# A low-rank adapter and a feed-forward network on one core: the adapter's second products in float32r from two parts

## The chip, the core and the metric

The kernel runs on one core of a Trainium2 chip. The core has TensorE (PE: products of matrices, with a separate weight load, PEld), VectorE (DVE), ScalarE (ACT), GpSimd (POOL) and SyncE (SP), which here only issues transfers. Data lie in SBUF, 128 partitions wide; products go to PSUM, 8 banks of 128 partitions by 512 float32. The engines run at the same time and wait for each other through semaphores; each one works off its own instructions in order.

The metric is the device time of one execution in microseconds, and for a kernel the median of several runs.

## The reference, cut to what matters

```
# x: (8, 256, 1024) float32; one adapter number per batch of 256 rows
B_sel = B[adapter_ids]; A_sel = A[adapter_ids]          # rank 16
Bx  = einsum('bnr', x, B_sel)                            # 1024 -> 16
c   = einsum('bno', Bx, A_sel)                           # 16 -> 1024, times 1.0
x_dq = fp8(clip(c / in_scale, -448, 448)) * in_scale
gate_out = x_dq @ (gate_w * gate_w_scale).T              # 1024 -> 2752
up_out   = x_dq @ (up_w * up_w_scale).T
hidden   = silu(gate_out) * up_out
h_dq     = fp8(clip(hidden / down_in_scale)) * down_in_scale
return x + h_dq @ (down_w * down_w_scale).T              # 2752 -> 1024
```

The weights are float32 that hold fp8 values. The adapter's two products decide what fp8 value each element of c rounds to, so they are made to float32's accuracy.

## The kernel before, in words

The 2048 rows (8 batches of 256) are four blocks t = 0 to 3 of 512 columns, two batches each, everything transposed: the 1024 features lie on 8 slices k of 128 partitions. The 2752 hidden features are 22 groups c of 128 (the last is half a group).

- **x and weights.** `load_x` (L381), `load_b` (L366), `load_a_two` (L373), the loop on `a_four` (L420) and `load_gate_up` (L391) issue transfers, nearly all on SP's queue, in the program's order: x of block 0 with its B and A; weights of groups 0 to 4 (`NFIRST = 5`), 1 MB each; B of block 1, x of block 1 in two pieces (7 slices, then 1), A of block 1 in four pieces of 16 rows; x of blocks 2 and 3, each followed by two B; the four A of blocks 2 and 3, 16 rows each; the rest. Eight semaphores are used in turn for these transfers.
- **B's product** (`times_b`). x is the moving operand, in float32, and one B of 16 columns (loaded as 32 columns, so the neighbours come along) the weights. Four products at a time use the four column groups of the array. Blocks 0 and 1 are done alone, with two batches, each halved, as the four (`two_times_b`: 128 columns each); blocks 2 and 3 together, with their four batches (`four_times_b`: 256 columns).
- **bm.** B's result is copied to SBUF. For blocks 0 and 1, bm has two versions of 64-row halves (`bm[:, other]`): VectorE copies one half of the rows, ScalarE the other, twice each (L517), so that each batch's A finds all columns. For blocks 2 and 3 it is one copy on VectorE (L557).
- **A's product** (`two_times_a`, `four_times_a`). Four products at a time use the four row groups of the array, with 32 rows of weights (16 of A, 16 of zeros) and 128 columns in block 1, and 16 rows and 256 columns in blocks 2 and 3. A call handles 4 accumulators of a PSUM bank each (two slices k by 256 columns); when they are complete, `round_to` evicts them to fp8 as xg, two on ScalarE (L529) and two on VectorE (L527).
- **Gate and up** (`gate_up(c, t)`): 8 products of 512 columns for gate, 8 for up (with `turns` in alternating pieces of two slices), then Silu on ScalarE (L610) and a fused multiply on VectorE (L611), which writes hid. `between` puts something between two of the 16 products. Groups 0 to 4 take block 0 first, then block 1, then blocks 2 and 3; groups 5 to 21 take all four blocks at a time.
- **Order.** TensorE's products go through `multiply` (L471) and keep the program's order, as do the copies to bm of blocks 0 and 1 and the checks `note_low_bits` and `note_squares` on ScalarE. Silu, fused multiply and the evictions are free: the framework's scheduler places them.
- **Around the change**, in the order of TensorE: `gate_up(4, 0)` is interrupted before its 13th product by block 1's B (`two_times_b(1)`), ends with its last 4, and `two_times_a(1)` follows, then `gate_up(0, 1)` in turns. `gate_up(3, 1)` is interrupted after 8 products by `four_times_b`, then `four_times_a` for the first two pairs of chunks (`pairs` 0, 1), `gate_up(4, 1)` interrupted after 8 by `four_times_a` for pairs 2 and 3; then groups 0 to 4 for blocks 2 and 3.
- **PSUM** is one pool of 8 banks, used by all of these in turn: a new accumulator waits for the readers of the one whose bank it takes.
- **Down** follows from group 22 on: 8 slices of the output, each with 21 products of hid and the tail, added to x and stored.

Of the kernel before, what the change touches and what calls it, by code (L numbers as in the profile page):

```python
# [8 lines left out]

F32 = mybir.dt.float32  # L10
BF16 = mybir.dt.bfloat16
FP8 = mybir.dt.float8e4
U16 = mybir.dt.uint16
I32 = mybir.dt.int32
AF = mybir.ActivationFunctionType
ALU = mybir.AluOpType
AX = mybir.AxisListType

P = 128
T = 2048  # L20
SEQ = 256
NB = 8
H = 1024
I = 2752
R = 16
NH = H // P
NI = (I + P - 1) // P
# [5 lines left out]
NFIRST = 5  # L33

BROW = NH * R + 8

KS = NH // 2
# [246 lines left out]
def adaln_ffn(  # L284
# [4 lines left out]
    aT: bass.AP,  # L289
    bT: bass.AP,  # L290
    a8: bass.AP,
    b8: bass.AP,
    w_gu: bass.AP,
    w_d: bass.AP,
# [3 lines left out]
    nc = tc.nc  # L298
    const = ctx.enter_context(tc.tile_pool(name="const", bufs=1))
    psum = ctx.enter_context(  # L300
        tc.tile_pool(name="psum", bufs=8, space=bass.MemoryType.PSUM)
    )
# [19 lines left out]
    kept = ctx.enter_context(tc.tile_pool(name="kept", bufs=1))  # L322
    wpool = ctx.enter_context(tc.tile_pool(name="w", bufs=5))
    outs = ctx.enter_context(tc.tile_pool(name="outs", bufs=3))
    hid = [kept.tile([P, T], FP8, name=f"hid{c}") for c in range(NI - 1)]


    hid_tail = kept.tile([P, 2, TB], BF16, name="hid_tail")
# [8 lines left out]
    with ExitStack() as fast:  # L337
# [17 lines left out]
        b_four = lora.tile([P, 4 * BROW + R], F32, name="b_four")  # L355
        a_four = lora.tile([P, H], F32, name="a_four")
        nc.gpsimd.memset(a_two[0], 0.0)
        nc.vector.memset(a_two[1], 0.0)
        for b, n in ((b_two[0], 2), (b_two[1], 2), (b_four, 4)):
            nc.vector.memset(b[:, n * BROW :], 0.0)  # L360

# [3 lines left out]
        def load_b(b, i, adapter, queue):  # L365
            queue.dma_start(  # L366
                out=b[:, i * BROW : (i + 1) * BROW], in_=b8[bass.ds(adapter * P, P), :]
            )

        def load_a_two(t, j, adapter, queue=nc.sync):  # L370
            for g in range(2):
                row = 32 * (2 * g + j) + R * j
                queue.dma_start(  # L373
                    out=a_two[t][row : row + R],
                    in_=a8[bass.ds(adapter * 2 * R + g * R, R), :],
                )

        def load_x(t, k):
            piece, first = x_of(x4, t, k)
# [27 lines left out]
        adapters = [adapter_of(2 + q, nc.sync) for q in range(6)]  # L407
        for j in range(2):
            load_b(b_two[1], j, adapters[j], nc.sync)
        for k in (0, 7):  # L410
            load_x(1, k)
        for j in range(2):
            load_a_two(1, j, adapters.pop(0))

        for t in (2, 3):
            load_x(t, 0)
            for q in (2 * t - 4, 2 * t - 3):
                load_b(b_four, q, adapters[q], nc.sync)
        for q in range(4):
            nc.sync.dma_start(  # L420
                out=a_four[32 * q : 32 * q + R], in_=aT[bass.ds(adapters[q] * R, R), :]
            )


        sc = b_two[0][:, NH * R : BROW]
# [44 lines left out]
        def multiply(*args, **kwargs):  # L470
            tc.keep_in_program_order(nc.tensor.matmul(*args, **kwargs))  # L471

        def pass_time(to, n, size=P):

            for i in range(n):
                multiply(
                    to[:, :size],
                    lhsT=zeros[:, :P],
                    rhs=zeros[:, :size],
                    start=(i == 0),  # L480
                    stop=(i == n - 1),
                )

        def times_b(bx, b, n, quads, between=None):


            for k in range(NH):
                for q, (i, row, t, cols) in enumerate(quads):
                    at = i * BROW + k * R - row
                    multiply(  # L490
                        bx[q][32 * q : 32 * (q + 1)],
                        lhsT=b[:, at : at + 32],
                        rhs=xs[t][:, k, cols],
                        start=(k == 0),
                        stop=(k == NH - 1),
                    )
                if between:
                    between(k)

        def two_times_b(t, between=None):  # L500


            n = SEQ // 2
            quads = [
                (j, R * j, t, slice(at, at + n))
                for half in range(2)
                for j in range(2)
                for at in (j * SEQ + half * n,)
            ]
            bx = [psum.tile([P, n], F32, tag="ps", name=f"bx{half}") for half in range(2)]  # L510
            times_b([bx[q // 2] for q in range(4)], b_two[t], n, quads, between)
            bm = lora.tile([P, 2, n], F32, tag="bm2", name="bm2", bufs=2)
            for other in range(2):
                for half, copy in enumerate((nc.vector.tensor_copy, nc.scalar.copy)):
                    to = half ^ other
                    tc.keep_in_program_order(
                        copy(  # L517
                            bm[64 * to : 64 * (to + 1), other],
                            bx[half][64 * half : 64 * (half + 1)],
                        )  # L520
                    )
            return bm

        def round_to(to, c, engine):
            scale = inv[:, GATE_IN : GATE_IN + 1]
            if engine is nc.vector:
                nc.vector.tensor_scalar(to, c, scale, None, ALU.mult, saturate=False)  # L527
            else:
                nc.scalar.activation(to, c, AF.Copy, scale=scale, saturate=False)  # L529

        def two_times_a(t, bm):


            n = SEQ // 2
            for part in range(2):
                cs = [psum.tile([P, 2, SEQ], F32, tag="ps", name=f"c{q}") for q in range(4)]
                for other, i in product(range(2), range(2)):
                    for q in range(4):
                        rows = slice(32 * q, 32 * (q + 1))
                        multiply(  # L540
                            cs[q][:, i, bass.ts(q // 2 ^ other, n)],
                            lhsT=a_two[t][rows, bass.ts(2 * part + i, P)],
                            rhs=bm[rows, other],
                            start=True,
                            stop=True,
                        )
                for q in range(4):
                    k = KS * part + 2 * (q // 2)
                    to = xg[t][:, k : k + 2, bass.ts(q % 2, SEQ)]
                    round_to(to, cs[q], nc.vector if q % 2 else nc.scalar)  # L550

        def four_times_b():
            quads = [(q, 0, 2 + q // 2, bass.ts(q % 2, SEQ)) for q in range(4)]
            bx = psum.tile([P, SEQ], F32, tag="ps", name="bx")
            times_b([bx] * 4, b_four, SEQ, quads)
            bm = lora.tile([P, SEQ], F32, tag="bm", name="bm", bufs=2)
            nc.vector.tensor_copy(bm, bx)  # L557
            return bm

        def four_times_a(bm, pairs):  # L560
            for i in pairs:
                cs = [psum.tile([P, 2, SEQ], F32, tag="ps", name=f"c{q}") for q in range(4)]
                for k in range(2):
                    for q in range(4):
                        rows = slice(32 * q, 32 * q + R)
                        multiply(
                            cs[q][:, k],
                            lhsT=a_four[rows, bass.ts(2 * i + k, P)],
                            rhs=bm[rows],
                            start=True,  # L570
                            stop=True,
                        )
                for q in range(4):
                    to = xg[2 + q // 2][:, 2 * i : 2 * i + 2, bass.ts(q % 2, SEQ)]
                    round_to(to, cs[q], nc.vector if q % 2 else nc.scalar)
# [5 lines left out]
        def gate_up(c, t, turns=(NH,), between=None):  # L581
# [23 lines left out]
            if tail:  # L605
                to = lora.tile([P, 2 * TB], FP8, tag="bm", name="tail", bufs=2)[half_of(t), :TB]
            else:
                to = hid[c][:, cols]
            g = work.tile([P, TB], F32, tag="g", name="g")
            nc.scalar.activation(g[rows], gates, AF.Silu, scale=gate_s[: gates.shape[0]])  # L610
            nc.vector.scalar_tensor_tensor(  # L611
                to,
                in0=ups,
                scalar=up_by_down[rows],
                in1=g[rows],
                op0=ALU.mult,
                op1=ALU.mult,
                saturate=False,
            )
            if tail:  # L620
                nc.vector.tensor_copy(hid_tail[half_of(t), t // 2], to)
            if t == (NTB - 1 if c < NFIRST else 1):
# [10 lines left out]

        warm = psum.tile([P, TB], F32, tag="ps", name="warm")
        pass_time(warm, 16, TB)
        bm = two_times_b(0, lambda k: pass_time(warm, 4) if k == 6 else None)
        pass_time(warm, 7)
        two_times_a(0, bm)
        gate_up(0, 0, turns=(2, 2, 2, 2))
        for c in range(1, NFIRST - 1):  # L640
            gate_up(c, 0)
        bms = []
        gate_up(NFIRST - 1, 0, between=(12, lambda: bms.append(two_times_b(1))))
        two_times_a(1, bms[0])
        gate_up(0, 1, turns=(2, 2, 2, 2))
        for c in range(1, NFIRST - 2):
            gate_up(c, 1)
# [238 lines left out]
```

## Time and profile before

| what | value |
| --- | --- |
| median of 3 runs | 475.71 us (475.62 to 475.85) |
| profiled execution, span from the first to the last instruction | 474.0 us |
| TensorE busy | 469.6 us, 99% |
| A's products of blocks 0 and 1, 128 records together | 4.3 us busy |
| A's products of blocks 2 and 3, 64 records | 4.1 us busy |
| B's products of blocks 0 and 1, 128 records; of 2 and 3, 64 records | 4.3 and 3.7 us busy |
| eviction of c, one of 128x512 | 0.688 us on ScalarE (L529), 0.745 on VectorE (L527) |
| copy to bm, 64x128 | 0.283 us on VectorE, 0.262 on ScalarE (L517) |
| copy to bm, 128x256 | 0.425 us on VectorE (L557) |
| Silu; fused multiply | 0.681 us (L610); 0.751 (L611) |
| GpSimd busy | 1.0 us in 7 instructions, all in the first 1.55 us |
| TensorE clock granted | 1.000 |

The median of the runs is 1.7 us more than the profiled span. A float32 product is recorded twice by the profiler, as two records. In the timeline a row gives the start, the time to the end of the last instruction merged into it, the engine, the line, the operation with its tiles and shapes, how many, and in brackets the idle time before it with what ended it. Ends of products are modelled, so neighbouring rows of PE overlap a little: the starts are to be read. Busy time of an engine that is not on the chain of waits costs nothing by itself.

### The profile page before, as it was taken

To read this page: it belongs to the slowest core of one execution; us is meant where nothing else is said; L and a number is where in the kernel's file an instruction comes from. 1 tells how busy PE (TensorE), PEld (TensorE's weight loads), DVE (VectorE), ACT (ScalarE), POOL (GpSimd) and SP (SyncE) were. 2 spreads that over 40 slices of the span, in tenths; PEclk is the share of its full clock that TensorE was granted. 3 is DMA by queue.
4 is the path that set the end of the run, shared out by engine and by line. 5 is a ranking of instruction groups with operands and counts; after the bars stand their busy time and mean duration, and the time that the engine had idled before them with its cause. 6 is when DMAs were issued, how large, how long until landed. Compare 5 with 4: busy or idle time off the path is not lost.

```text
span 474.0 us, 6007 instructions
## 1 busy us (share of the span) xinstructions
PE 469.6 (99%) x2514; PEld 217.1 (46%) x2514; DVE 105.6 (22%) x163; ACT 192.5 (41%) x249; POOL 1.0 (0%) x7
## 2 busy tenths in 40 slices
PE   8999999999999999999999999999999999999997
PEld 5454544444444444444444444444444444444444
DVE  2332521212212121222212121232120121031031
ACT  2332438995555745443354544359212022021000
POOL 0000000000000000000000000000000000000000
DMA  8995023322222112222210121133335255163031
GB/s 316 416 406 153 1 90 115 153 89 90 89 89 90 54 45 80 90 89 89 90 57 36 41 62 56 61 100 106 115 135 162 66 184 160 28 212 110 3 116 67
DMA packets 13781, 53.45 MB, mean 113 GB/s; under 512 B 1650, under 2 KB 2930, under 8 KB 10802
## 3 DMA queue, kind: packets, MB, share of 16 engines
q1 hardware_dynamic: 13536, 52.86, 31.8%
q8 instruction: 21, 0.34, 0.3%
q10 hardware_dynamic: 210, 0.14, 0.1%
q14 instruction: 14, 0.11, 0.1%
HBM read 44.60 MB, written 8.39 MB: 112 GB/s over the span
## 4 chain that ended last, share of the span: by engine, by line
PE 96%; DMA 2%; ACTq 0%; ACT 0%; issue 0%; DVE 0%
PE y L471 62%; PE yd L471 32%; DMA w_gu<-w_gu 1%; PE c L471 1%; PE bx L471 1%; DMA a<-a 1%; ACT L307 0%; ACTq L373 0%; ACTq L306 0%; ACTq L366 0%; DVE o L696 0%; ACTq L363 0%; PE count L471 0%
## 5 line engine op out<-in xcount | busy, mean ns | idle before, releaser
L471 PE MATMUL y<-xg,w_gu 128*128 128x512 fp8e4 x1376 | 298.2, 379 | 0.1
L471 PEld LDWEIGHTS <-w_gu 128*128 128x128 bf16 x1376 | 134.1, 98 | 162.8 <-issue 1.3
L471 PE MATMUL yd<-hid,w_d 128*128 128x512 fp8e4 (+2 forms) x693 | 146.0, 373 | 0.0
L610 ACT ACTIVATE g<-y,gate_s 128x512 f32<-128x512 f32 (+1 forms) x88 | 59.8, 681 | 136.3 <-PE y L471 136.3
L611 DVE SCALAR_TENSOR_TENSOR hid<-y,up_by_down,g 128x512 fp8e4<-128x512 f32 x84 | 63.1, 751 | 219.4 <-PE y L471 161.6
L471 PEld LDWEIGHTS <-w_d 128*128 128x128 bf16 x693 | 66.6, 98 | 79.0 <-issue 1.7
L457 ACT ACTIVATE junk<-w_d 128x1408 bf16<-128x1408 uint16 (+1 forms) x16 | 21.2, 1324 | 88.5 <-DMA w_d<-w_d 88.4
L696 DVE SCALAR_TENSOR_TENSOR o<-yd,down_s,x 128x512 f32<-128x512 f32 x28 | 20.0, 748 | 107.3 <-PE yd L471 92.5
L457 ACT ACTIVATE junk<-w_gu 128x2048 bf16<-128x2048 uint16 (+1 forms) x22 | 41.0, 1863 | 0.0
L464 ACT ACTIVATE junk<-hid 128x2048 bf16<-128x2048 fp8e4 x21 | 40.0, 1904 | 0.4
L464 ACT ACTIVATE junk<-xg 128x2048 bf16<-128x2048 fp8e4 x8 | 15.3, 1909 | 0.3
L529 ACT ACTIVATE xg<-c,inv 128x512 fp8e4<-128x512 f32 x16 | 9.7, 688 | 8.6 <-PE c L471 8.6
L527 DVE TENSOR_SCALAR xg<-c,inv 128x512 fp8e4<-128x512 f32 x16 | 10.9, 745 | 2.8 <-PE c L471 2.8
L471 PE MATMUL warm<-zeros 128*128 128x512 bf16 (+1 forms) x27 | 6.6, 404 | 1.2 <-DVE zeros L309 1.2
L696 DVE SCALAR_TENSOR_TENSOR o<-yd,down_s,xg 128x512 f32<-128x512 f32 (+2 forms) x5 | 3.2, 644 | 12.3 <-PE yd L471 12.3
L517 ACT COPY bm<-bx 64x128 f32<-64x128 f32 x4 | 1.0, 262 | 9.2 <-PE bx L471 9.2
L471 PEld LDWEIGHTS <-zeros 128*128 128x128 bf16 x27 | 2.6, 117 | 4.8 <-issue 3.1
L471 PE MATMUL bx<-x,b 128*32 128x128 f32 x128 | 4.3, 276 | 0.1
L471 PE MATMUL c<-bm,a 32*128 32x128 f32 x128 | 4.3, 277 | 0.0
L457 ACT ACTIVATION_READ_ACCUMULATOR junk<-w_gu 128x1 f32 x22 | 4.2, 191 | 0.0
L471 PEld LDWEIGHTS c<-bm,a 32*128 32x128 f32 x128 | 3.9, 186 | 0.5 <-ACT bm L517 0.4
L471 PE MATMUL yd<-hid_tail,w_dt 64*128 64x512 bf16 (+1 forms) x32 | 4.1, 377 | 0.0
(47 smaller groups left out, 41.0 us busy)
## 6 DMA issues: line engine op xcount, KB each, us to landing
w_gu<-w_gu SPq DMA_DIRECT2D x20, 1024.0 KB, 4.8
outT<-o SPq DMA_DIRECT2D x31, 256.0 KB, 2.2
w_d<-w_d SPq DMA_DIRECT2D x8, 704.0 KB, 4.9
w_d<-w_d SPq DMA_DIRECT2D x8, 640.0 KB, 3.9
x<-x SPq DMA_DIRECT2D x2, 2048.0 KB, 11.3
x<-x SPq DMA_DIRECT2D x1, 1792.0 KB, 13.1
w_gu<-w_gu SPq DMA_DIRECT2D x3, 512.0 KB, 4.2
x<-x SPq DMA_DIRECT2D x2, 512.0 KB, 3.9
```

Of the source, the lines that this page charges most:

```text
L457: nc.scalar.activation(junk_like(w), low(w), AF.Copy, accum_out=lows[:rows, column : column + 1])
L464: nc.scalar.activation(junk_like(q), q, AF.Square, accum_out=squares[:rows, column : column + 1])
L471: tc.keep_in_program_order(nc.tensor.matmul(*args, **kwargs))
L517: copy(bm[64 * to : 64 * (to + 1), other], bx[half][64 * half : 64 * (half + 1)],)
L527: nc.vector.tensor_scalar(to, c, scale, None, ALU.mult, saturate=False)
L529: nc.scalar.activation(to, c, AF.Copy, scale=scale, saturate=False)
L610: nc.scalar.activation(g[rows], gates, AF.Silu, scale=gate_s[: gates.shape[0]])
L611: nc.vector.scalar_tensor_tensor(to, in0=ups, scalar=up_by_down[rows], in1=g[rows], op0=ALU.mult, op1=ALU.mult, saturate=False,)
L696: nc.vector.scalar_tensor_tensor(o, in0=y, scalar=down_s, in1=x, op0=ALU.mult, op1=ALU.add)
```

## The change

[...] Block 0 stays as it was.

- A is loaded twice into 32 rows (two new inputs, `a8_twice` and `a_twice`, hold the copies). GpSimd makes parts of it (`split`): rows whose number has bit 4 clear get A rounded, the others A minus A rounded, by a multiplication with 0 or -1 per row (`minus`, from an iota and two small VectorE instructions) and an addition.
- B is doubled on GpSimd (`twice`), so that Bx comes out in both 16-row halves of each row group; `times_b` takes these as weights, 32 columns as before.
- bm is Bx rounded to float32r, and `rest` is Bx minus bm, also in float32r. For block 1: each of VectorE and ScalarE copies its own 64 rows, VectorE makes two subtractions, ScalarE copies four halves to the other rows. For blocks 2 and 3: one copy and one subtraction on VectorE.
- A's product is then the sum of two products with 32 rows and 256 columns, one with bm and one with rest, accumulated in PSUM (`times_a_parts`).
- The transfers of A of block 1 (now 32 rows each) stand ahead of x of block 1. The memset of that tile on VectorE goes.
- Silu and fused multiply of groups 0 to 4 keep the program's order (`keep_in_program_order`), and with them what depends on the order of their queue.
- The tiles for the parts use the places of hid 9 to 20, which are written later.

```diff
-        nc.vector.memset(a_two[1], 0.0)
+        def load_a_twice(a, q, src, part):
+            nc.sync.dma_start(
+                out=a[32 * q : 32 * (q + 1)], in_=src[bass.ds(part * 2 * R, 2 * R), :]
+            )
...
+        for j in range(2):
+            adapter = adapters.pop(0)
+            for g in range(2):
+                load_a_twice(a_two[1], 2 * g + j, a8_twice, adapter * 2 + g)
         for k in (0, 7):
             load_x(1, k)
-        for j in range(2):
-            load_a_two(1, j, adapters.pop(0))
...
         for q in range(4):
-            nc.sync.dma_start(
-                out=a_four[32 * q : 32 * q + R], in_=aT[bass.ds(adapters[q] * R, R), :]
-            )
+            load_a_twice(a_four, q, a_twice, adapters[q])
+        lane = const.tile([P, 1], I32, name="lane")
+        nc.gpsimd.iota(lane, pattern=[[0, 1]], base=0, channel_multiplier=1)
+        nc.vector.tensor_scalar(lane, lane, R, None, ALU.bitwise_and)
+        minus = const.tile([P, 1], F32, name="minus")
+        nc.vector.tensor_scalar(minus, lane, -1.0 / R, None, ALU.mult)
+        def split(a, parts):
+            nc.gpsimd.tensor_scalar(parts, a, minus, None, ALU.mult)
+            nc.gpsimd.tensor_tensor(parts, a, parts.bitcast(F32), ALU.add)
+        def twice(b, n, name, slot):
+            tiles = []
+            for i in range(n):
+                to = in_place_of_hid(slot - i, [P, NH, 2, R], F32, f"{name}{i}")
+                row = b[:, i * BROW : i * BROW + NH * R].rearrange("p (k r) -> p k r", r=R)
+                for copy in range(2):
+                    nc.gpsimd.tensor_copy(to[:, :, copy], row)
+                tiles.append(to.rearrange("p k c r -> p (k c r)"))
+            return lambda i, k, row: tiles[i][:, 2 * R * k : 2 * R * (k + 1)]
...
+        b_twice = [twice(b_two[1], 2, "b_twice", NI - 2)]
+        split(a_two[1], a_parts[0])
+        b_twice.append(twice(b_four, 4, "b_four_twice", NI - 4))
+        for i in range(2):
+            split(a_four[:, bass.ts(i, H // 2)], a_parts[1 + i])
...
+        def two_times_b_in_parts():
...
+            times_b([bx[q // 2] for q in range(4)], b_twice[0], n, quads_of_two(1, 0))
+            bm = lora.tile([P, 2, n], F32R, name="bm_parts")
+            rest = in_place_of_hid(NI - 11, [P, 2, n], F32R, "rest")
+            held = tc.keep_in_program_order
+            own = [slice(64 * half, 64 * (half + 1)) for half in range(2)]
+            for half, copy in enumerate((nc.vector.tensor_copy, nc.scalar.copy)):
+                held(copy(bm[own[half], half], bx[half][own[half]]))
+            for half in range(2):
+                held(
+                    nc.vector.tensor_tensor(
+                        rest[own[half], half],
+                        bx[half][own[half]],
+                        bm[own[half], half].bitcast(F32),
+                        ALU.subtract,
+                    )
+                )
+            for part, half in ((bm, 1), (bm, 0), (rest, 0), (rest, 1)):
+                held(nc.scalar.copy(part[own[1 - half], half], part[own[half], half].bitcast(F32)))
...
+        def times_a_parts(bms, a, at):
+            cs = [psum.tile([P, 2, SEQ], F32, tag="ps", name=f"c{q}") for q in range(4)]
+            for bm, i in product(bms, range(2)):
+                for q in range(4):
+                    rows = slice(32 * q, 32 * (q + 1))
+                    multiply(
+                        cs[q][:, i],
+                        lhsT=a[rows, bass.ts(at + i, P)],
+                        rhs=bm[rows],
+                        start=bm is bms[0] and i == 0,
+                        stop=bm is bms[-1] and i == 1,
+                    )
+            return cs
...
         def four_times_b():
...
             nc.vector.tensor_copy(bm, bx)
-            return bm
+            rest = in_place_of_hid(NI - 13, [P, SEQ], F32R, "rest4")
+            nc.vector.tensor_tensor(rest, bx, bm.bitcast(F32), ALU.subtract)
+            return bm, rest
...
+            last = [
+                nc.scalar.activation(g[rows], gates, AF.Silu, scale=gate_s[: gates.shape[0]]),
+                nc.vector.scalar_tensor_tensor(...),
+            ]
+            if c < NFIRST:
+                for instruction in last:
+                    tc.keep_in_program_order(instruction)
```

## The prediction

> **What bounds the kernel now.** I read the page's chain of waits first, then the timeline from 28 to 62 us, then the DMA issues.
>
> ```profile
> span 474.0 us, 6007 instructions
> PE 469.6 (99%) x2514; PEld 217.1 (46%) x2514; DVE 105.6 (22%) x163; ACT 192.5 (41%) x249; POOL 1.0 (0%) x7
> ...
> PE 96%; DMA 2%; ACTq 0%; ACT 0%; issue 0%; DVE 0%
> ```
>
> The same chain in order of time (start, length, what):
>
> ```profile
> 57.30 264.29 PE y L471 x1224
> 321.59 121.08 PE yd L471 x570
> ```
>
> TensorE bounds it, 96% of the chain, and after 57.3 us it is held by nothing but its own products until 442, so the change is worth what it shifts the start of the first product of block 2. All it touches on the path lies in two places. Block 1 first:
>
> ```profile
> 28.13 0.69 ACT L610 ACTIVATE g<-y,gate_s 128x512 f32<-128x512 f32 x1 [2.77 <-PE y L471]
> 28.88 1.95 PE L471 MATMUL bx<-x,b 128*32 128x128 f32 x64
> 30.77 1.04 PE L471 MATMUL y<-xg,w_gu 128*128 128x512 fp8e4 x4
> 30.87 0.60 DVE L517 COPY bm<-bx 64x128 f32<-64x128 f32 x2 [3.65 <-PE bx L471]
> 30.93 0.55 ACT L517 COPY bm<-bx 64x128 f32<-64x128 f32 x2 [2.12 <-PE bx L471]
> 31.74 2.14 PE L471 MATMUL c<-bm,a 32*128 32x128 f32 x64
> 31.91 0.75 DVE L611 SCALAR_TENSOR_TENSOR hid<-y,up_by_down,g 128x512 fp8e4<-128x512 f32 x1 [0.45 <-PE y L471]
> 32.93 2.42 ACT L529 ACTIVATE xg<-c,inv 128x512 fp8e4<-128x512 f32 x4 [1.45 <-PE c L471]
> 32.97 2.73 DVE L527 TENSOR_SCALAR xg<-c,inv 128x512 fp8e4<-128x512 f32 x4 [0.31 <-PE c L471]
> 33.81 12.26 PE L471 MATMUL y<-xg,w_gu 128*128 128x512 fp8e4 x56
> ```
>
> See that y at 33.81 starts as VectorE's first eviction ends (32.97 + 0.74 = 33.71), and that A's 64 records end there too: product and eviction are equally late. See also that the Silu of this group (28.13) was done before B's product. Blocks 2 and 3:
>
> ```profile
> 51.42 2.11 PE L471 MATMUL c<-bm,a_four 16*128 16x256 f32 x32
> 51.60 0.75 DVE L611 SCALAR_TENSOR_TENSOR hid<-y,up_by_down,g 128x512 fp8e4<-128x512 f32 x1 [1.45 <-PE y L471]
> 52.59 2.42 ACT L529 ACTIVATE xg<-c,inv 128x512 fp8e4<-128x512 f32 x4 [5.79 <-PE c L471]
> 52.63 2.73 DVE L527 TENSOR_SCALAR xg<-c,inv 128x512 fp8e4<-128x512 f32 x4 [0.28 <-PE c L471]
> 53.46 1.90 PE L471 MATMUL y<-xg,w_gu 128*128 128x512 fp8e4 x8
> 55.29 1.61 PEld L471 LDWEIGHTS c<-bm,a_four 16*128 16x128 f32 x32 [0.42 <-issue]
> 55.30 2.01 PE L471 MATMUL c<-bm,a_four 16*128 16x256 f32 x32
> ```
>
> See that four products (one round over the four row groups, 256 columns) take 2.04/4 = 0.51 us, in two records each, and that evictions follow each other every 0.58 us on ScalarE (2.42 less one of 0.688, by 3) and every 0.66 on VectorE (2.73 less 0.744, by 3).
>
> **The change, part by part.**
>
> *A's products.* Removed: in block 1, 8 rounds of 128 columns (2.07 us); in blocks 2 and 3, 8 rounds of 256 (3.98). Added: 8 and 16 rounds of 256 columns in float32r. No row shows float32r. Bounds for one round: 0.109 us (half the step of a 512-column product, 13.12 us for 60 in the chain) and 0.51 (float32 at the same width). Nearest is one float32 record at 128 columns with the same 32x128 weights: 2.07/16 = 0.129, with as much streaming as 256 columns at one per step. I take 0.13 us.
> The Trainium skill (FP8 and Floating Point Precision, TensorE Precision Notes) gives true float32 four passes and a reduced one that reads it cut; a quarter of 0.51 is an estimate of 0.128, which would leave the sum as it is.
>
> *Block 1, who is late next.* VectorE now does one copy of 64x128 (0.283) and two subtractions of that size; ScalarE five copies instead of two, since the other halves of bm and rest are copied from SBUF. In the built order Silu, fused multiply and evictions keep program order, so the Silu of (4, 0) moves from 28.13 to behind these copies, the fused multiply (L611) behind it, and VectorE's evictions behind that. Work: ScalarE starts at 30.93 as before; five copies at the step of 0.287 (0.55 - 0.262) end at 32.34; two of them wait for results just made, some 0.05 each: 32.45. Silu to 33.14, multiply 33.18 to 33.93, first VectorE eviction to 34.67 (I let the two overlap by nothing). y starts 0.09 after, as before: 34.76, against 33.81: +0.95. The four accumulators of the second half reuse the banks of the group's two outputs and wait for the same multiply; their 3.25 remaining rounds (0.42) end at 34.4, before that eviction, so A's faster product is worth nothing here. Turns of 0.87 us per two slices then hide the later evictions (0.66 apart). Bounds: +0.6, if three more copies at 0.262 are all that delays it and the multiply overlaps; +1.3, if each dependent copy waits 0.1.
>
> *Blocks 2 and 3.* The subtraction on VectorE (nearest: the copy of 128x256, 0.425) ends at about 50.6 behind 8 products of y that run to 51.42: free; without them 0.45. First pair of chunks 51.42 to 51.94. The second pair's last accumulator reuses the bank freed by the multiply at 51.60 + 0.75: 52.42, then 3.25 rounds: 52.84 (before: 53.44). y to 54.68. Third pair: its last round ends, as an eviction sees it, 0.2 after the last start, 55.3. The fourth pair's last accumulator needs the bank of the third pair's first (in the built order the Silu that would free another stands behind all evictions): ScalarE 55.3 to 55.99, then 3.25 rounds: 56.5. Before, y went on at 57.24: -0.74. With 0.109: -0.95. With the float32 record of 256 columns (0.25) as a round: +0.7. PSUM write contention between the row groups is unseen; I take -0.65.
>
> *DMA.* The four pieces of A for block 1 double to 64 KB and move ahead of x; they pass x's two pieces, and B, x and A of blocks 2 and 3 keep their order. SP's queue issues a transfer when the one eight before it has landed (A's third and fourth went out at 20.62 and 23.17, released by w_gu); x takes the third one's place, at 20.62 instead of 15.10. w_gu still flows until 23.1, so the stream doesn't run dry. Landings are in order: b 23.6 (14.71 + 8.9), x 28.2 (15.10 + 13.1), its last slice 28.87, A 29.07, 29.33, 29.52: 0.20 to 0.26 for each 32 KB. The a_four pieces of 64 KB landed 0.26 apart. Four pieces cost 0.64 us by bytes at 0.41 MB/us, 1.0 at 0.26, 1.6 at twice 0.20 (twice the rows), 2.1 at most. x lands at 28.84, 29.2, 29.8 or 30.3, and TensorE wants it at 28.88. I take 0.33 a piece: 29.5, +0.62 (bounds 0 and 1.4). Behind this wait stand B's product, the last four of y and all of the chain above. x's last slice lands at 30.2, wanted at 30.6 + 0.6.
>
> *GpSimd.* B doubled (four copies) and A's split (two of 128x512, nearest row the memset, 0.529) begin after 24.6 and have to end by 28.9 and 31.7: hidden. For blocks 2 and 3, b lands near 42.5, wanted at 46; a_four near 44.5, wanted at 51.4.
> The Trainium skill (GPSIMD Engine Reference, Elementwise side-by-side) would put such work on VectorE: 4497 ns for a two-input add of 2048 columns, some 1.1 us for 512 as an estimate; with that the split ends near 27.5, and the sum stays.
>
> *iota.* A code reload and an iota stand on GpSimd ahead of all this, and two small VectorE operations wait for them, queued ahead of block 0's bm copies at 9.59. GpSimd is free at 1.55. No row shows the reload. Bounds: 0, and 0.3 us of a DMA stream that is full from 2 us on (what queue 14 fetched for instructions, 0.11 MB, at 0.37), shifting w_gu, for which TensorE waits at 15.8. I take 0.15.
> The skill's same page (Instruction dispatch) has about 6 us for a fresh library's first call: iota at 7.6 as an estimate, still before 9.59, price nothing.
>
> **The sum:** 0.95 - 0.65 + 0.62 + 0.15 = +1.07 us. The span goes from 474.0 to 475.0; the runs' median is 1.7 us over the span, so 475.71 becomes **476.8**. About 0.2% (0.95 us) is what a measurement of this kernel can tell from no change.
>
> **Rivals.** (1) x isn't late: A's pieces cost their bytes alone, and the 0.68 us between 28.2 and 28.88 swallows it; the wait decides only from 0.68 us of delay on. For it: full DMA share throughout; against: 0.2 us per 32 KB. 475.71 + 0.45 = 476.2, not slower by the measure above. (2) Evictions don't bind, because other banks are free or ScalarE's copies are short: blocks 2 and 3 give the full 3.98 - 2.08 = 1.9, block 1 loses 0.0: -1.9 + 0.62 + 0.15 = -1.1, 474.6, faster. Against it: the order as built. (3) float32r streams like a float32 record: blocks 2 and 3 at +0.7 instead of -0.65: 478.1. For it: rows have no other four-byte price; against: the format is shorter. (4) The reload holds iota past 9.59, or its fetch delays x of block 0: each us beyond goes to the end; at 11 us, 478.2. For it: DMA is full at that time; against: 8 us of room.
>
> **Chances.** Forecast 0.45 (476.4 to 477.3, some 0.13 of it inside 0.2%), rival 1 0.20, 2 0.12, 3 0.10, 4 0.13. So faster 0.12; within 0.2% 0.20 + 0.13 = 0.33; slower 0.55. Range: from 475.0, short of most of rival 2, to 478.4, with rivals 3 and 4 at their centre.
>
> **What would show it.** B's product of block 1 starting at 29.5 behind a DMA of x, not at 28.9; the Silu of (4, 0) after five ScalarE copies near 32.4; first y of block 1 some 4.0 us after B's end, not 3.04; rounds of c at 0.13 us; a gap in c of the fourth pair that ends with a ScalarE eviction; bm copies of block 0 still at 9.59. Wrong it is if c rounds take 0.25 us or more, or if y follows c at once in blocks 2 and 3.

## The result, and the profile after

| kernel | median of the runs | lowest to highest | profiled execution, span |
| --- | --- | --- | --- |
| before | 475.69 us (5 runs) | 475.56 to 475.85 | 474.0 us |
| changed | 477.57 us (5 runs) | 476.94 to 478.16 | 476.1 us |

The ratio is 1.0039, with a 95% interval of [1.0026, 1.0051]: the change costs 1.9 us, 0.8 more than forecast. The page of the changed kernel, its busy times and the shares of its chain of waits:

```profile
PE 468.7 (98%) x2482; PEld 215.8 (45%) x2482; DVE 105.9 (22%) x166; ACT 193.5 (41%) x252; POOL 12.5 (3%) x26
...
PE 92%; DMA 5%; ACT 1%; DVE 0%; ACTq 0%; issue 0%; SPq 0%; DVEq 0%
```

TensorE is busy 0.9 us less than before (468.7 against 469.6), and the span is 2.1 us longer: what is lost is waiting, and the chain now goes through DMA, ScalarE and VectorE. The same chain in order of time (start, length, what; times in us):

```profile
20.72 9.52 DMA x<-x
...
30.38 2.01 PE bx L523 x64
...
32.42 0.27 ACT bm_parts L595
...
33.87 0.69 ACT g L712
...
34.59 0.76 DVE hid L713
...
35.40 0.73 PE c L523 x12
36.13 12.19 PE y L523 x56
...
54.66 0.73 PE c L523 x12
...
59.40 264.29 PE y L523 x1224
```

Read it downward. Block 1's B product (`bx`) waits for x, which went out at 20.72 and took 9.5 us; before, it started at 28.88 without a wait. Then the chain leaves TensorE: five ScalarE copies from 32.42 to 33.85, then the Silu `g`, then the fused multiply `hid`. The second half of A's products (`c` at 35.40) waits for a bank that this multiply frees, and block 1's first y comes behind them. The line at 54.66 is the second pair of chunks in blocks 2 and 3, which waits for a multiply too. The last line is the long run of y that ends the early part; it started at 57.30 before and starts at 59.40 now, and these 2.1 us are the whole difference of the spans.

The timeline has the same stretch by starts:

| stretch (start to start) | before | changed | difference |
| --- | --- | --- | --- |
| w_gu's wait in block 0: y goes on | 15.82 | 15.91 | +0.09 |
| B of block 1 starts | 28.88 | 30.38 | +1.50, with the +0.09 |
| B of block 1 to its first y | 4.93 | 5.68 | +0.75 |
| first c of blocks 2 and 3 to the y after the fourth pair | 5.82 | 5.65 | -0.17 |

1.50 + 0.75 - 0.17 = 2.08. Before, the last row ends at this line:

```profile
57.24 5.14 PE L471 MATMUL y<-xg,w_gu 128*128 128x512 fp8e4 x23
```

In the changed kernel it begins at 53.68 and ends behind the third and fourth pair of chunks (timeline: start, time to the end of the last one, engine and line, operation, in brackets the idle time before it and what ended it):

```profile
53.68 0.51 PE L523 MATMUL c<-bm,a_parts 32*128 32x256 f32 x8
...
57.16 0.51 PE L523 MATMUL c<-bm,a_parts 32*128 32x256 f32 x8
57.50 0.41 PE L523 MATMUL c<-rest,a_parts 32*128 32x256 f32 x8
57.73 0.28 PE L523 MATMUL c<-bm,a_parts 32*128 32x256 f32 x3
57.93 2.66 ACT L614 ACTIVATE xg<-c,inv 128x512 fp8e4<-128x512 f32 x4 [1.06 <-PE c L523]
58.67 0.50 PE L523 MATMUL c<-bm,a_parts 32*128 32x256 f32 x5 [0.65 <-ACT xg L614]
58.90 0.50 PE L523 MATMUL c<-rest,a_parts 32*128 32x256 f32 x8
59.33 2.98 PE L523 MATMUL y<-xg,w_gu 128*128 128x512 fp8e4 x13
```

Three products of the fourth pair go out, and the next one waits until ScalarE has evicted the third pair's first bank (57.93 + 0.69 = 58.62). Call products that follow each other without a wait a streak. Inside one, a round of four products takes 0.117 us from start to start (57.50 to 57.73, two rounds): the format is as fast as it was taken to be. A float32 round, of which half as many are needed, takes 0.43 inside a streak of the kernel before, two records 0.216 us apart (six steps from 55.62 to 56.91); the 0.51 of the prediction is a whole streak's mean, with its ends and a short wait. For a streak has fixed prices. Its first two rounds take 0.34 and not 0.23 (57.16 to 57.50), 0.11 more, and the step from its last round to y is 0.21, some 0.1 more. A wait inside a round adds to that: the 13 products that are left here, three rounds and a quarter, go out in four steps (58.67, 58.90, 59.01, 59.13).

### The profile page after: what moved, and what is told of

The parts are those of the page before. It is cut to its first block, busy times and chain, and to the rows that moved or that the text cites. A ratio compares the mean times of both kernels' runs of the same rounds, so it can differ in the third digit from the quotient of the medians.

```text
span 476.1 us, 5967 instructions
## 1 busy us (share of the span) xinstructions
PE 468.7 (98%) x2482; PEld 215.8 (45%) x2482; DVE 105.9 (22%) x166; ACT 193.5 (41%) x252; POOL 12.5 (3%) x26
## 4 chain that ended last, share of the span: by engine, by line
PE 92%; DMA 5%; ACT 1%; DVE 0%; ACTq 0%; issue 0%; SPq 0%; DVEq 0%
PE y L523 59%; PE yd L523 31%; DMA w_gu<-w_gu 2%; DMA x<-x 2%; PE bx L523 1%; DMA a<-a 1%; PE c L523 1%; DVE hid L713 0%; ACT L310 0%; SPq L408 0%; ACT g L712 0%; ACT xg L614 0%; ACT bm_parts L606 0%; ACTq L385 0%; ACTq L309 0%
## 5 line engine op out<-in xcount | busy, mean ns | idle before, releaser
L713 DVE SCALAR_TENSOR_TENSOR tail<-y,up_by_down,g 64x512 fp8e4<-64x512 f32 x4 | 3.0, 756 | 4.9 <-ACT g L712 4.8
L516 ACT ACTIVATION_READ_ACCUMULATOR junk<-hid 128x1 f32 x21 | 3.9, 187 | 0.0
L523 PE MATMUL bx<-x,b_four_twice 128*32 128x256 f32 x64 | 3.7, 380 | 0.0
```

The source lines that it names most:

```text
L516: nc.scalar.activation(junk_like(q), q, AF.Square, accum_out=squares[:rows, column : column + 1])
L713: nc.vector.scalar_tensor_tensor(to, in0=ups, scalar=up_by_down[rows], in1=g[rows], op0=ALU.mult, op1=ALU.mult, saturate=False,),
```

## The experiments

Ratios are to the kernel before, run beside them on the same chip (medians 475.85, 475.79 and 475.80 for the first four, the next four and the last three), with their 95% intervals; they are not quotients of the medians, and where a few executions were long (478.68 us in "A behind, halves, free") the ratio is the higher. Medians of different sets can differ by more than the kernels do: the changed kernel itself had 477.57 in one and 477.04 in another. All are single edits of the changed kernel or combinations of them. The table shows starts in the profiled execution of each.

| kernel | B of block 1 | B to y | c to y, blocks 2 and 3 | last y | median | ratio |
| --- | --- | --- | --- | --- | --- | --- |
| before | 28.88 | 4.93 | 5.82 | 57.24 | | |
| changed | 30.38 | 5.68 | 5.65 | 59.33 | 477.57 | 1.0039 [1.0026, 1.0051] |
| A behind x | 28.77 | 6.32 | 5.65 | 58.35 | 477.25 | 1.0034 [1.0021, 1.0047] |
| order free | 29.55 | 4.89 | 4.99 | 57.05 | 475.51 | 0.9993 [0.9984, 1.0002] |
| half of A | 29.21 | 5.68 | 5.65 | 58.16 | 476.63 | 1.0014 [1.0005, 1.0023] |
| blocks 2 and 3 only | 28.93 | 5.23 | 5.68 | 57.45 | 475.96 | 1.0005 [0.9994, 1.0015] |
| A between, halves, free | 29.00 | 5.27 | 5.00 | 56.88 | 475.27 | 0.9993 [0.9985, 1.0002] |
| blocks 2 and 3 only, free | 28.92 | 4.92 | 4.99 | 56.45 | 474.88 | 0.9981 [0.9972, 0.9990] |
| A behind, halves, free | 28.88 | 5.76 | 5.00 | 57.25 | 475.83 | 1.0011 [0.9998, 1.0024] |
| half of A, free | 29.11 | 4.89 | 5.00 | 56.62 | 475.18 | 0.9991 [0.9982, 1.0] |
| changed, again | 29.53 | 5.69 | 5.66 | 58.49 | 477.04 | 1.0028 [1.0017, 1.0039] |
| half by half, free | 28.93 | 5.08 | 5.00 | 56.62 | 475.19 | 0.9988 [0.9979, 0.9997] |
| Silu of (4, 0) free | 29.50 | 4.90 | 5.65 | 57.66 | 476.24 | 1.0012 [1.0003, 1.0021] |

The column "last y" is the y after the fourth pair. Its shift from 57.24 is the shift of the median to within 0.3 us in every row, so the three columns before it hold the matter.

**A behind x.** The order of the transfers is put back to x first.

```diff
-        for j in range(2):
-            ...load_a_twice(a_two[1], ...)
         for k in (0, 7):
             load_x(1, k)
+        for j in range(2):
+            ...load_a_twice(a_two[1], ...)
```

> The four pieces of A of block 1 go back behind the two pieces of x. My theory (x waits for the transfer of A's pieces, 1.41 us of the 2.1): B's product of block 1 starts near 28.95 us, as in the kernel before, not at 30.38. A then lands near 30.1, and GpSimd's split (1.57 + 1.26 us in the changed kernel) ends near 33.0, over 1 us after bm is ready; but the first VectorE eviction stands behind Silu and multiply until about 33.9 anyhow, so y still starts 5.7 us after B's start. Median 1.0 to 1.4 us under the changed kernel: 476.2 to 476.6. Rival (the slowdown is in block 1's longer chain alone, x's wait is an accident of one profile): the start moves, the median stays within 0.4 us of 477.6.

B's product started at 28.77, so the wait for x was the doing of A's place. But the first y came 6.32 us after it, not 5.7, and the median missed the 476.2 to 476.6 expected: 477.25 lies between the two medians of the changed kernel. Timeline of this kernel:

```profile
30.51 1.57 POOL L453 TENSOR_SCALAR a_parts<-a,minus 128x512 fp32r<-128x512 f32 x1 [5.99 <-DMA a<-a_twice]
...
32.16 1.26 POOL L454 TENSOR_TENSOR a_parts<-a,a_parts 128x512 fp32r<-128x512 f32 x1
...
33.48 0.51 PE L523 MATMUL c<-bm_parts,a_parts 32*128 32x256 f32 x8 [1.78 <-POOL a_parts L454]
```

A now lands at 30.3, GpSimd's two instructions take 2.8 us, and c waits 1.78 us for them, past the point where the held multiply had been expected to hide them. The early place of A buys the split its time: one wait was exchanged for another.

**Order free.** The lines that keep Silu and fused multiply in the program's order are taken out; the scheduler then puts the Silu of (4, 0) ahead of the ScalarE copies, and that of (4, 1) ahead of the evictions of the last two pairs.

```diff
-            if c < NFIRST:
-                for instruction in last:
-                    tc.keep_in_program_order(instruction)
```

> Silu and fused multiply of groups 0 to 4 are left to the scheduler again, which puts the Silu of (4, 0) ahead of the copies and that of (4, 1) ahead of the last evictions. My theory (the held Silu makes VectorE's first eviction late): first y of block 1 starts 4.9 us after B's product instead of 5.68, and c of the fourth pair waits less, y following near 5.0 us after the first c of blocks 2 and 3 instead of 5.65. Together -1.3 to -1.5 us: median 476.1 to 476.3. Rival (ScalarE's five copies make the chain long, whatever the order): block 1 stays at 5.5 us or more, the median gains at most 0.5 us.

4.89 and 4.99 us, as expected; the median, 475.51, is lower than the 476.1 to 476.3 expected. The order that the change holds costs 0.79 us in block 1 and 0.66 in blocks 2 and 3; the rest of the gain (59.33 to 57.05) is that x came 0.83 earlier in this execution. With no order held the kernel is level with the one before.

**Half of A.** Of each 32-row piece of A for block 1 only 16 rows are loaded, in the place ahead of x, and the lower rows are zero; the lower half of A's parts is thus missing from c.

```diff
+        nc.vector.memset(a_two[1], 0.0)
...
-                load_a_twice(a_two[1], 2 * g + j, a8_twice, adapter * 2 + g)
+                q, part = 2 * g + j, adapter * 2 + g
+                nc.sync.dma_start(
+                    out=a_two[1][32 * q : 32 * q + R], in_=a8_twice[bass.ds(part * 2 * R, R), :]
+                )
```

> A of block 1 is loaded ahead of x, but only the 16 rows for the rounded part, 32 KB a piece; the rows for the remainder are zero, so block 1's c lacks A's lower part. The number of pieces and the issue times stay (x goes out near 20.7). Theory a (A's bytes and small packets ahead of x cost the time): x lands 0.5 to 0.8 us earlier, B's product starts at 29.6 to 29.9, median 476.8 to 477.1. Theory b (x is late because it is issued at 20.7 and not at 15.1): the start stays at 30.2 to 30.5 and the median within 0.3 us of 477.6.

x went out as late as in the changed kernel (20.62), and TensorE hardly waited for it: its y run to 29.11, and B started at 29.21. So the late issue of x, 20.6 instead of 15.1, costs at most some 0.2 us here, and theory b fell. Theory a named the cause but not the size: start and median came below its ranges. The median is 0.94 us under the changed kernel's first one, and 0.41 under the one of its second set of runs (below). The doubled bytes, or packets, ahead of x are worth some 0.4; these two were not told apart, and the rest of the 0.94 differs between executions of one kernel (below).

**Blocks 2 and 3 only.** Block 1 is made in float32 as before, its transfers, copies and B as there, with the order still held. Of the edit:

```diff
-        gate_up(NFIRST - 1, 0, between=(12, lambda: bms.append(two_times_b_in_parts())))
-        two_times_a_parts(bms[0])
+        gate_up(NFIRST - 1, 0, between=(12, lambda: bms.append(two_times_b(1))))
+        two_times_a(1, bms[0])
...
```

> Block 1 as in the kernel before (float32 A behind x, 128 columns, bm copied twice each), blocks 2 and 3 in float32r; Silu and multiply of groups 0 to 4 still held. My theory: no wait for x; the held Silu costs block 1 some 0.25 us, since two copies and not five stand ahead of it; blocks 2 and 3 give 0.1 to 0.2. Median 475.5 to 475.9, equal to the kernel before. Rival (blocks 2 and 3 give more than the profile shows): 475.2 or less.

Block 1 takes 5.23 us with only two copies ahead of the held Silu: 0.30 above before, without any float32r in it. Blocks 2 and 3 gain 0.14. Both came about as expected, and the median, 475.96, just above its range. All but 0.1 us of the loss thus hangs on block 1's part of the change, x's wait among it, and of what float32r saves in the products of blocks 2 and 3 little arrives.

**A between x's pieces, split in halves, order free.** With the edit of "Order free", and:

```diff
+        load_x(1, 0)
         for j in range(2):
             ...load_a_twice(a_two[1], ...)
-        for k in (0, 7):
-            load_x(1, k)
+        load_x(1, 7)
...
-        split(a_two[1], a_parts[0])
+        for i in range(2):
+            at = bass.ts(i, H // 4)
+            split(a_two[1][:, at], a_parts[0][:, at])
```

> A's loads of block 1 stand between x's seven slices and its last one, the split is done in halves of 256 columns, and the Silu and multiply of the held chunks may be moved again. Theory (both losses, the wait for x and the held Silu, are removable and apart): B's product of block 1 starts at about 28.9 as before, the first half of A is split by about 31.5, before the shares are ready (2.9 us after B's start), block 1's first y 4.9 us after B's start, the four-block products 5.0 us from first c to the next y: 0.8 under before, 475.05 us (474.7 to 475.4). Rival (x's bytes still share the way with A's, whatever their order): the last slice of x, or A's split, is late by 0.4 or more, and the time is 475.5, as with the order free alone.

x was in time (B at 29.00), blocks 2 and 3 took 5.00 from c to y, but B to y took 5.27: A landed at 29.9, and GpSimd made both multiplications before the first addition, so that c waited 0.73 us for the first half. The median, 475.27, lies in theory's range all the same.

**Blocks 2 and 3 only, order free.** The edits of these two experiments together.

> Block 1 is as in the kernel before, blocks 2 and 3 in float32r, and nothing holds the Silu and multiply. Theory: block 1 costs what it did before (4.93 us from B's start to the first y, B's start at 28.9), the four-block products 5.0 us in place of 5.82: 475.05 us (474.8 to 475.3). Rival (with the order held and free alike the four-block products gain only 0.15, because the evictions of c set their pace and not their order): 475.7.

Both of theory's numbers came: 4.92 and 4.99. It is the fastest version of the study, 0.19% under the kernel before with an interval that excludes 1. Its third and fourth pair, in the timeline:

```profile
54.93 0.51 PE L520 MATMUL c<-bm,a_parts 32*128 32x256 f32 x8
55.04 0.69 ACT L709 ACTIVATE g<-y,gate_s 128x512 f32<-128x512 f32 x1 [0.39 <-PE y L520]
...
55.71 2.42 ACT L611 ACTIVATE xg<-c,inv 128x512 fp8e4<-128x512 f32 x4
...
56.45 3.84 PE L520 MATMUL y<-xg,w_gu 128*128 128x512 fp8e4 x17
```

The Silu at 55.04 frees a bank while ScalarE has nothing to evict yet, and no wait for an eviction stands in c of the fourth pair any more. From the first c of this third pair to y it is 1.52 us, against 2.17 in the changed kernel, where the Silu stands behind the evictions.

**A behind x, split in halves, order free.**

> A's loads of block 1 stand behind both pieces of x, the split is done in halves of 256 columns, and the Silu and multiply may be moved. With A landing at 30.3 as in the run with A behind x and 1.45 us for half a split, the first half is ready at 31.8, where the shares of B are ready at about 31.8 too: c waits for the split 0 to 0.3 us. Theory: B's start at 28.9, first y 4.9 to 5.2 after it, 475.05 to 475.4 us. Rival (the cost of a split is per instruction and not per column): c waits 1 us or more, and the time is 476 or above.

The theory fell: c waited 1.22 us and the median is 475.83, because here too GpSimd ran both multiplications first (1.83 us) before the first addition (0.70). The rival's reason, a price per instruction and not per column, fell as well: a half took 0.92 and 0.73 us, a whole 1.57 and 1.26.

**Half of A, order free.**

> As the run with half of A's rows loaded (32 KB pieces ahead of x; the lower 16 rows of each quarter are zero and so add nothing, which leaves the float32r products a copy of what the lower rows held), but with the Silu and multiply free to move. If the wait for x and the held order are apart and add: half of A was worth 0.94 with the order held; the order was worth 2.06; of the wait for x the free kernel had only 0.4 us left in its profile, so 475.0 us (474.7 to 475.3), and B's start at 28.9 to 29.1. If the two are one cost seen twice: 475.5, as with the order free alone.

In the profile the costs are apart: B at 29.11 with 0.17 us of waiting left for x, and 4.89 and 5.00 us as with the order free alone. The median, 475.18, is where that theory puts it and 0.33 under the order free alone, but in another set of runs: the ratios, 0.9991 and 0.9993, do not tell the two kernels apart.

**The changed kernel again.**

> The changed kernel as it is, beside the other runs. Theory (the wait for x of block 1 is no fixed price: it was 1.41 us in the profile of the changed kernel, 0.4 in that of the kernel with the order free, and it differs from execution to execution): B's product of block 1 starts between 29.3 and 30.5, the time is 476.9 to 477.6 us, and the executions lie wider apart (1 us or more) than those of the kernel with x not late (0.5 us). Rival (the wait is a fixed 1.4 us that freeing the order happened to shorten): B at 30.3 again, 477.6 us, executions within 0.5 us.

Timeline of this execution:

```profile
29.53 1.96 PE L523 MATMUL bx<-x,b_twice 128*32 128x128 f32 x64 [0.47 <-DMA x<-x]
```

The first profiled execution has 1.34 us in this bracket. B started 0.85 us earlier here, the last y 0.84 earlier, and all else was the same (5.69 and 5.66). So the wait for x is not a fixed price of this kernel. GpSimd's split, which starts as A lands, began at 25.55 in the first execution and at 25.58 in this one: A's pieces were through at the same time, and the 0.85 us arose behind them. But its runs in this set lay within 0.22 us of each other, not 1 us apart as the theory had it: the price differs between one set of runs and another (477.57 and 477.04 us), and within the first set (476.94 to 478.16). What decides it was not found.

**Half by half, order free.** As the kernel with A between x's pieces, with GpSimd's instructions held in the order multiply, add, multiply, add.

```diff
-            nc.gpsimd.tensor_scalar(parts, a, minus, None, ALU.mult)
-            nc.gpsimd.tensor_tensor(parts, a, parts.bitcast(F32), ALU.add)
+            tc.keep_in_program_order(nc.gpsimd.tensor_scalar(...))
+            tc.keep_in_program_order(nc.gpsimd.tensor_tensor(...))
```

> As the run with A's loads between x's pieces, but GpSimd finishes the first half of the split before it begins the second (0.92 + 0.73 us after A's landing at 29.9 to 30.0, so 31.6 to 31.75). Theory: c of block 1 no longer waits for the split (0.7 us of it there), starts at 31.9, first y 4.9 to 5.0 us after B's start at 29.0, the four-block products 5.0 us: 474.9 us (474.7 to 475.2), no better than blocks 2 and 3 alone in float32r. Rival (A's landing is as uncertain as x's and decides in half of the executions): 475.3, as before.

c started at 31.78 with no wait, but the second half ended at 33.28, and the second c pair waited 0.37 us for it: 5.08 and not 4.9 to 5.0. That pair then runs without a wait inside it, up to y:

```profile
33.33 0.51 PE L525 MATMUL c<-bm_parts,a_parts 32*128 32x256 f32 x8 [0.37 <-POOL a_parts L454]
...
33.67 0.40 PE L525 MATMUL c<-rest,a_parts 32*128 32x256 f32 x8
...
34.01 12.26 PE L525 MATMUL y<-xg,w_gu 128*128 128x512 fp8e4 x56
```

The first two rounds take 0.34 us and so do the last two, against 0.23 inside a streak. The time, 475.19, is within the range given, and above the kernel that leaves block 1 in float32.

**Only the Silu of (4, 0) free.**

```diff
-            if c < NFIRST:
+            if c < NFIRST and (c, t) != (NFIRST - 1, 0):
```

> The changed kernel with the Silu and multiply of chunk 4 in block 0 alone free to move; the scheduler then puts that Silu ahead of the five copies on ScalarE and leaves all else. Theory (block 1's loss is that Silu behind the copies): first y of block 1 4.9 us after B's start in place of 5.68, the four-block products 5.65 us as in the changed kernel: 0.75 under the changed kernel of the same call. Rival (the copies are not what holds it; the shares or the split set the end): 5.4 us or more after B's start, 0.3 under at most.

Its block 1 in the timeline:

```profile
32.47 0.75 DVE L713 SCALAR_TENSOR_TENSOR hid<-y,up_by_down,g 128x512 fp8e4<-128x512 f32 x1
...
33.02 0.51 PE L523 MATMUL c<-rest,a_parts 32*128 32x256 f32 x8
...
33.59 2.72 DVE L612 TENSOR_SCALAR xg<-c,inv 128x512 fp8e4<-128x512 f32 x4 [0.37 <-PE c L523]
...
34.40 12.26 PE L523 MATMUL y<-xg,w_gu 128*128 128x512 fp8e4 x56 [0.40 <-DVE xg L612]
```

One instruction moved past five copies is worth 0.80 us of the median (477.04 to 476.24, run side by side) and 0.79 from B to y; blocks 2 and 3 stay at 5.65. The multiply now ends at 33.2, before the first accumulators are complete: VectorE waits 0.37 us for c, where c's second half waited for VectorE.

## Why the prediction was right in kind, and where its sizes failed

The forecast of a slower kernel held, and by the mechanism named: a loss in block 1 behind a held Silu, a loss in front of it for x, and a small gain in blocks 2 and 3. By its terms:

- **Block 1, +0.95: it was +0.75.** Counted from B's start, the Silu was forecast at 3.57 us and came at 3.49, the first VectorE eviction at 5.05 and came at 4.88 (the multiply and the eviction behind it follow each other every 0.67, not 0.75), y at 5.88 and came at 5.68. The run with one Silu free shows the cause as named. The last step was a tie, where the forecast had the second half of A's products done 0.27 us before VectorE's first eviction: its last 13 products took 0.66 us and not 0.42, the chain of waits goes through them to y at 36.06, and the eviction ended at 36.00, about as long before y as in the run with one Silu free, where y does wait for it (34.34 and 34.40).
- **Blocks 2 and 3, -0.65: it was -0.17, and -0.14 to -0.17 in every run that holds the order. This is the step that failed.** The chain of waits in it was right: the second pair behind the multiply, the fourth behind a ScalarE eviction. The mis-sized terms are the streaks. "3.25 rounds (0.42)" after each of the two waits took 0.67 and 0.66 (54.66 to 55.33, 58.67 to 59.33), and the eviction of the third pair began 0.77 after its first product, not 0.62. 0.25 + 0.24 + 0.15 is 0.64 more, less 0.07 in the other pieces, against a shortfall of 0.48 from the value taken, which stood 0.09 on the safe side of its own working. I had priced rounds alone, at 0.13, and that price was generous (0.117 inside a streak). Left out were 0.11 at the start of each streak, some 0.1 before the y behind it, and that 3.25 rounds go out in four steps: 4 times 0.117 plus 0.2 is 0.67. The float32 streaks of the kernel before have such ends too (0.32 us to the second record and 0.33 from the last to y, 0.216 between), so the rows of before held them.
- **x of block 1, +0.62 with bounds of 0 and 1.4: 1.4 in the first profiled execution, 0.5 to 0.6 in the others with the same transfers** (waits of 1.34, and 0.47, 0.38 and 0.58 in the changed kernel again, with the order free and with one Silu free). The value taken was near the later three; the first lies at the upper bound. That what A puts ahead of x does it, and not x's later issue, half of A shows for some 0.4 us; the first execution's further 0.85 stays open.
- **iota and its reload, +0.15: at most 0.09.** The iota ran at once, at 1.57 us, and the two VectorE instructions behind it were done at 7.10; block 0's bm copies started at 9.67, not 9.59, but behind B's last products, so that the 0.09 can't be put down to the iota:

```profile
1.57 0.13 POOL L443 IOTA lane<- 128x1 int32 x1
```

With 0.75 in place of 0.95, -0.17 in place of -0.65 and 1.50 for x and block 0 together in place of 0.77, the 1.07 becomes 2.08. In the second execution it is 0.65 + 0.76 - 0.16 = 1.25, beside a median that was 1.24 higher. That this is near 1.07 is partly luck: block 1 was priced 0.19 too high and x with the iota 0.12 too high, which covers most of the 0.49 by which the gain of blocks 2 and 3 was priced too high.

Of the rivals, x that isn't late fell with B at 29.5 and later, and evictions that don't bind with the fourth pair's wait; float32r like a float32 record fell with rounds of 0.117 us, and a late iota with the line above. What would have shown the forecast wrong (rounds of 0.25, or y at once behind c) didn't come. GpSimd's covers held: the split for block 1 ended at 28.5 and was wanted at 33.2, those for blocks 2 and 3 ended near 51.0 and were wanted at 53.7. Its price did not: two instructions, taken at 0.529 each from the memset, took 1.57 and 1.26, which cost nothing here and decided the run with A behind x.

The Trainium skill (FP8 and Floating Point Precision, TensorE Precision Notes) gives float32 four passes; the quarter of a float32 round estimated from it, 0.128 us, is near the measured 0.117, and a quarter of the 0.43 inside a streak, 0.108, a little under it. The skill's page GPSIMD Engine Reference (Instruction dispatch) has about 6 us for a fresh library's first call: no row here shows a reload, and the iota took 0.13 us straight behind a memset, so this trace doesn't show it.

## What to carry to other kernels

Faster products are worth little where the next thing waits for evictions and banks: of some 1.6 us that blocks 2 and 3 saved in products (eight rounds of 0.43 us replaced by sixteen of 0.117), 0.17 reached the end, and 0.83 once the Silu that frees a bank could go ahead of the evictions. An order held for one reason should be checked for what it puts last on each queue; here it cost 1.45 us in two places, more than the 0.83 that the new format earned without it. A short streak of products is priced with its ends, not by its rounds alone. Inputs moved ahead in a full stream of transfers take their time from the next user; where that one is on the path, leaving the work out (block 1 in float32) was the better trade, while another place for A (between x's pieces) showed no gain beyond the noise over freeing the order alone.

## What the runs showed of the hardware that was not expected

A change from full products to a streak of small ones (32 rows by 256 columns, four row groups) and back costs some 0.2 us beyond the rounds, 0.11 at the start and some 0.1 at the end, in float32r and in float32 alike. On GpSimd a multiplication of 128x512 by one value per partition took 1.57 us, more than the addition of two such tiles, 1.26 (the lines stand at A behind x).

And a stream of transfers that is full by its share carries less where A's pieces are in it. From 22 to 24 us, by stretches (engines' busy times, granted clock, DMA share, GB/s), first the kernel before:

```profile
22.00:24.00 2.00, 2.00 (x11) 0.88 (x9) 0.75 (x1) 0.00 (x0) 0.00 (x0) 1.00 1.07 453
```

and the changed kernel:

```profile
22.00:24.00 2.00, 2.00 (x11) 0.94 (x10) 0.75 (x1) 0.00 (x0) 0.00 (x0) 1.00 1.09 327
```

The share is the same, and the bytes are 28% fewer. The kernel with half of A moved as little (301 GB/s in this stretch) and had x in time, and with A behind x it moved 450 there and 347 from 26 to 28 us, so the dip goes with A's place and doesn't say how late x will be. Nor is it known why one program's x took 9.52 us from issue to landing in one execution and 8.67 in another.
